# A four-layer macaron model on one Trainium2 core: ends of mixtures by tile, products ahead of the gates, and the first batch of layer 1's attention begun inside the mixture before it

## The chip, the core and the metric

The kernel runs on one core of one Trainium2 chip. The core has a matrix engine (PE, with its weight loads shown as PEld), a vector engine (DVE), a scalar engine (ACT), a general engine (POOL, or GpSimd) and a queue that issues most of the DMAs (SP). They run side by side and meet through semaphores; DMAs of all queues share 16 DMA engines. On-chip memory is SBUF (128 partitions) and PSUM (8 banks of 128 x 512 fp32 here), into which PE writes. The metric is the device time of one launch in microseconds (us); lower is better. Time before is the median of three runs.

## The reference, cut to what matters

The state x has 4 batches of 512 tokens of width 128, all in fp32. Every one of four layers adds half a mixture, an attention, and half a mixture again. In layers 1 and 2 the mixture is computed for every expert, in layers 0 and 3 by sending tokens to experts with a capacity.

```python
x = x + 0.5 * _L0_ffn_ref(_layernorm(x), ...)    # top 1, capacity 320, each layer: ffn, attn, ffn
x = x + _L0_attn_ref(_layernorm(x), ...)
x = x + 0.5 * _L0_ffn_ref(_layernorm(x), ...)
x = x + 0.5 * _L1_ffn_ref(_layernorm(x), ...)    # layer 1: the one that the change is mostly about
x = x + _L1_attn_ref(_layernorm(x), ...)
x = x + 0.5 * _L1_ffn_ref(_layernorm(x), ...)
...                                              # layer 2: dense mixture, scan, dense mixture
x = x + 0.5 * _L3_ffn_ref(_layernorm(x), ...)    # top 2, capacity 512
x = x + _L3_attn_ref(_layernorm(x), ...)
x = x + 0.5 * _L3_ffn_ref(_layernorm(x), ...)

def _L1_ffn_ref(x):                    # 8 experts of width 64, 2 shared ones (together 128 wide)
    shared = silu(x @ ws_gate.T) * (x @ ws_up.T) @ ws_down.T
    scores = sigmoid(x @ gate_weight.T)
    w, idx = top_k(scores, 2); w = 2.5 * w / (w.sum(-1) + 1e-20)
    return shared + sum over the two of w * expert(x)

def _L1_attn_ref(x):                   # 16 heads; scores are a product of two low-rank score matrices
    A1 = einsum('bnhr,bmhr->bhnm', q1, k1)   # rank 4
    A2 = einsum('bnhr,bmhr->bhnm', q2, k2)   # rank 8
    attn = softmax(causal(A1 * A2 * 32 ** -0.5))
    return (attn @ v) @ Wo.T + bo
```

## The kernel before

**Order of work.** The program is one straight sequence. Outside of marked blocks a scheduler arranges each engine's instructions by itself, from the order of the source and the dependences; inside blocks of `tc.manual_schedule` the named engines keep the order of the source. All attentions are such blocks (PE, DVE, ACT and POOL), and the chain from layer 1's second mixture to layer 3's first routing (the generator `behind`) is one for POOL alone. Work of two pairs of batches is interleaved by `skewed`: each stage is a generator that yields at step ends, and the second pair starts a given number of rounds after the first (5 for layer 1's first mixture, 8 for `behind`).

**Norms.** `norms` (from L155) takes statistics per tile of 128 tokens on DVE, `rs`, `rstd` (a power), and `off` on POOL (L164, L165, L168, L169) and the normalised tile on ACT, POOL or DVE (L174, L176, L178), as its argument `on` says. `normed_T` (L1039) uses it with "scalar", so ACT, for pairs of batches in the mixtures of layers 1 and 2.

**Mixtures with a capacity** (`Mixture`, layers 0 and 3: f00, f01, f30, f31). `experts` (from L414) goes over 8 experts. For each it makes the hidden rows `h` (L479, L483, L484), and then for every piece of 128 rows four products into one PSUM bank `po` (L514), a bias on DVE (`biased`, L496), a scale on ACT (L501) and an indirect scatter to DRAM by POOL (L502). `at_once` is how many pieces the bias takes at a time: all of them (`whole`), for the last expert one. `combine` (L524) loads the scattered rows of each batch (L529) and adds them to x (L530); in the last one the answer of each batch is sent out right behind (L1545).

**Layer 1's mixture** (`l1_ffn`, from L1075), for a pair of batches: normalise and turn (`normed_T`), gate scores (`scored`, Sigmoid at L1081), routing on DVE (`route`, `without`, up to the gates `comb` at L1094), the gates turned and written to DRAM (`to_rows`, L1065) and fetched back as rows replicated over partitions, 512 KB a piece, two per batch (`cb`, L1102, from SP). Then for each batch five steps k, the shared experts first: gate and up products on PE (L1127, L1128), Silu on ACT (L1130), times up on DVE (L1131), in the other steps times the gate rows on DVE (L1133), and, two steps behind, the down products of the step k - 2 (L1115). The result is added to x at L1140. The first step is of the shared experts, the other four of two experts each.

**Layer 1's attention** (`l1_attn`, from L1143). `begin(b)` normalises and turns batch b, makes three factor matrices (L1165), writes them to DRAM (L1172 once, L1176 eight times) and makes the values; `fetch` loads the factors replicated for a group of four heads (L1193), and `project` multiplies them to q on DVE and k on POOL (L1200), so that scores are one product per head (L600). Before the first score the tiles `vpad` for padded values are set to 0 and 1 on POOL (`padded_values`, L571, called at L796), and in layer 3 also the tiles `low` (L801).

**Layer 2's preparation** (`prep_l2`) turns `wo` of each expert on PE and copies the result on ACT (L1246, L1252), beside other work.

The main sequence is at L1466 to L1545.

Of the kernel before, what the change touches and what calls it, by code (L numbers as in the profile page):

```python
# [9 lines left out]
FP = mybir.dt.float32  # L10
# [31 lines left out]
def kernel(ctx: ExitStack, tc: tile.TileContext, a: dict, out: bass.AP):  # L42
# [109 lines left out]
    def norms(srcs, dsts, tag, on="vector", fine=False):  # L152
# [18 lines left out]
        for t in range(g):  # L171
            src, dst = srcs[t // NT][:, t % NT, :], dsts[t // NT][:, t % NT, :]
            if on == "scalar":
# [63 lines left out]
    class Mixture:  # L237
# [180 lines left out]
        def experts(self, w, beside=None):  # L418
# [3 lines left out]
            with tc.tile_pool(name=f"moe_{self.tag}", bufs=2) as pool:  # L422
# [47 lines left out]
                for e in range(E):  # L470
# [20 lines left out]
                    po = bank(f"o{tag}").rearrange("p (s d) -> p s d", d=D)  # L491
# [3 lines left out]
                    def biased(m, t0, t1):  # L495
                        nc.vector.tensor_tensor(  # L496
                            o[:m, t0:t1, :], po[:m, t0:t1, :], bc_mid(b2[:m, e, :], [m, t1 - t0, D]), ALU.add
                        )
# [11 lines left out]
                    at_once = 1 if e == E - 1 else whole  # L510
                    for s in range(per):
                        m = min(P, cap - s * P)
                        for c in range(NC):
# [4 lines left out]
                        if s >= whole or (s + 1) % at_once == 0:  # L518
                            first = s if s >= whole else s + 1 - at_once
                            biased(m, first, s + 1)  # L520
# [49 lines left out]

    def padded_values(pool):  # L571
        vpads.clear()
        for i in range(2):
            v = pool.tile([P, NT, NH, SLOT], FP, name=f"vpad{i}", tag=f"vpad{i}", bufs=1)
            nc.gpsimd.memset(v, 0.0)
            nc.gpsimd.memset(v[:, :, :, HD : HD + 1].rearrange("p t h o -> p (t h o)"), 1.0)
            vpads.append(v)

    def attention(pool, tag, begin, project, residual, owT, added, after=None, beside=(), fetch=None):
# [216 lines left out]
        padded_values(pool)  # L796
        if not added:
            lows = []
            for i in range(2):
                low = pool.tile([P, NT, P], FP, name=f"low{i}_{tag}", tag=f"low{i}", bufs=1)  # L800
                nc.gpsimd.memset(low, 0.0)  # L801
                lows.append(low)
# [236 lines left out]
    def normed_T(pool, bs, tag):  # L1039

        ns = [work.tile([P, NT, D], FP, name=f"n{b}_{tag}", tag="n", bufs=3) for b in bs]
        yield from norms([xs[b] for b in bs], ns, tag, "scalar")
# [32 lines left out]
    def l1_ffn(pool, i, bs):  # L1075
# [3 lines left out]
        plg = scored(nTs, l1["gate"], tag)  # L1079
        sc = pool.tile([P, G, E], FP, name=f"sc_{tag}", tag="sc1")  # L1080
        nc.scalar.activation(sc, plg, AF.Sigmoid)  # L1081
# [12 lines left out]
        nc.vector.tensor_tensor(comb, comb, bc(total, [P, G, E]), ALU.mult)  # L1094
        yield
# [11 lines left out]
        order = [NC] + list(range(NC))  # L1107
        for x, b in enumerate(bs):
            po = bank(f"o{b}_{tag}").rearrange("p (t d) -> p t d", d=D)
            hs = []  # L1110

            def down(k):

                for t in range(NT):
                    nc.tensor.matmul(  # L1115
                        po[:, t, :],
                        hs[k][:, t * P : (t + 1) * P],
# [5 lines left out]
            for k, c in enumerate(order):  # L1123
                gw = l1["wg"][:, c * P : (c + 1) * P] if c < NC else l1["sg"]
                uw = l1["wu"][:, c * P : (c + 1) * P] if c < NC else l1["su"]
                ps = pair(f"gu{c}_{b}_{tag}")
                nc.tensor.matmul(ps[0], gw, nTs[x], start=True, stop=True)  # L1127
# [454 lines left out]
```

## Time and profile before

| what | us |
|---|---|
| median of 3 runs | 1516.54 |
| lowest and highest of them | 1515.89, 1519.27 |
| the profiled execution | 1538.12 |
| its span, first to last instruction | 1536.2 |

The profiled execution is one run of its own, and 1.4% above the median. Its span is 1.9 us shorter than its time. Busy shares of its span:

| engine | busy us | share |
|---|---|---|
| PE | 1282.4 | 83% |
| DVE | 852.7 | 56% |
| ACT | 713.5 | 46% |
| POOL | 653.9 | 43% |

By the timeline the span divides into these stages:

| from to, us | stage |
|---|---|
| 60 to 112 | experts of layer 0's first mixture |
| 127 to 340 | layer 0's attention |
| 340 to 430 | routing and experts of layer 0's second mixture |
| 430 to 455 | norm and routing of layer 1's first mixture, end of layer 2's preparation |
| 455 to 514 | layer 1's first mixture |
| 514 to 533 | start of layer 1's attention, up to the first score |
| 533 to 755 | layer 1's attention |
| 757 to 832 | layer 1's second mixture |
| 832 to 1045 | layer 2, routing of layer 3's first mixture |
| 1045 to 1101 | experts of layer 3's first mixture |
| 1101 to 1416 | layer 3's attention |
| 1445 to 1518 | experts of layer 3's second mixture |
| 1518 to 1536 | loads of its rows, answers |

A line of the timeline has the start, the busy time, the engine, the line of the source, the operation, the tiles written and read, their shapes, the number of instructions, and in brackets the idle time of the engine before it with what ended it. A line of a group of instructions has the engine, the operation, tiles and shapes, the count, then the busy time of all and the mean in ns of one, then the idle time before them and what ended it.

### The profile page before, as it was taken

To read this page: it belongs to the slowest core of one execution; us is meant where nothing else is said; L and a number is where in the kernel's file an instruction comes from. 1 tells how busy PE (TensorE), PEld (TensorE's weight loads), DVE (VectorE), ACT (ScalarE), POOL (GpSimd) and SP (SyncE) were. 2 spreads that over 40 slices of the span, in tenths; PEclk is the share of its full clock that TensorE was granted. 3 is DMA by queue.
4 is the path that set the end of the run, shared out by engine and by line. 5 is a ranking of instruction groups with operands and counts; after the bars stand their busy time and mean duration, and the time that the engine had idled before them with its cause. 6 is when DMAs were issued, how large, how long until landed. Compare 5 with 4: busy or idle time off the path is not lost. (4 is left out here: it accounts for less than half of the span.)

```text
span 1536.2 us, 28724 instructions
## 1 busy us (share of the span) xinstructions
PE 1282.4 (83%) x10645; PEld 824.8 (54%) x10645; DVE 852.7 (56%) x2832; ACT 713.5 (46%) x1487; POOL 653.9 (43%) x776
## 2 busy tenths in 40 slices
PE   4788999996969689999799877829599999997493
PEld 3465666764756456667567656617443334332272
DVE  5226777663335367857456545434277787773342
ACT  1235877871443266777633232103236555564041
POOL 4356767761510287868401111544630224202253
PEclk9898999996979799999999868859879999999597
DMA  8420240002414575331050000032104000000233
GB/s 253 109 62 8 78 171 9 9 18 76 138 46 98 145 234 161 101 119 55 3 111 1 1 0 1 29 90 70 56 21 167 15 11 5 15 2 14 77 84 103
DMA packets 100659, 106.20 MB, mean 69 GB/s; under 512 B 9084, under 2 KB 73832, under 8 KB 100520
## 3 DMA queue, kind: packets, MB, share of 16 engines
q1 hardware_dynamic: 93864, 91.16, 20.6%
q0 software_dynamic: 6656, 13.22, 2.7%
q8 instruction: 84, 1.38, 0.4%
q14 instruction: 55, 0.45, 0.1%
HBM read 62.49 MB, written 41.85 MB: 68 GB/s over the span
## 5 line engine op out<-in xcount | busy, mean ns | idle before, releaser
L632 POOL TENSOR_SCALAR sc_a<-sc_a,top_a 128x128 f32<-128x128 f32 (+3 forms) x256 | 275.4, 1091 | 82.7 <-DVE top_a L617 54.5
L600 PE MATMUL s_a<-k_a,q_a 32*128 32x512 f32 (+3 forms) x1536 | 264.9, 549 | 20.8 <-DMA k_a<-fac_a 13.8
L709 ACT ACTIVATE w_a<-t_a 128x512 f32<-128x512 f32 x256 | 140.5, 596 | 121.8 <-PE t_a L600 89.8
L645 PE MATMUL t_a<-ident,sc_a 128*128 128x128 f32 x1280 | 173.0, 281 | 7.3 <-DVE top_a L621 6.9
L600 PE MATMUL t_a<-ql_a,k_a 32*128 32x512 f32 x512 | 168.7, 646 | 0.3 <-DVE low_a__12648 L689 0.2
L502 POOL DMA_INDIRECT res_f<-y_f,back_f x112 | 109.2, 975 | 139.6 <-ACT y_f L501 105.1
L645 PEld LDWEIGHTS t_a<-ident,sc_a 128*128 128x128 f32 x1280 | 143.8, 144 | 44.3 <-issue 16.6
L634 ACT ACTIVATE sc_a<-sc_a,top_a 128x128 f32<-128x128 f32 (+3 forms) x256 | 135.3, 575 | 27.8 <-DVE top_a L621 27.3
L600 PEld LDWEIGHTS s_a<-k_a,q_a 32*128 32x128 f32 x1536 | 92.7, 189 | 92.9 <-issue 41.3
L654 ACT ACTIVATE w_a<-t_a 128x256 f32<-128x256 f32 (+2 forms) x192 | 94.1, 526 | 70.3 <-PE t_a L645 70.0
L408 POOL DMA_INDIRECT disp_f<-n_f,to_f x96 | 95.1, 991 | 54.4 <-issue 36.7
L514 PE MATMUL o_f<-w_l,h_f 128*128 128x128 f32 (+1 forms) x896 | 113.4, 279 | 3.8 <-DVE o_f L496 1.7
L514 PEld LDWEIGHTS o_f<-w_l,h_f 128*128 128x128 f32 (+1 forms) x896 | 103.1, 184 | 15.1 <-DVE back_f L464 4.4
L479 PE MATMUL h_f<-dT_f,w_l 128*128 128x320 f32 (+1 forms) x256 | 105.1, 547 | 2.8 <-ACT dT_f L457 2.8
L164 POOL TENSOR_SCALAR rs_f<-mv_f 128x4 f32<-128x4 f32 (+1 forms) x23 | 5.8, 250 | 229.0 <-DVE mv_f L161 228.6
L667 PE MATMUL acc_a<-w_a,vpad 128*32 128x128 f32 x2560 | 98.0, 279 | 0.3 <-ACT w_a L654 0.3
L689 DVE TENSOR_REDUCE low_a__12648<-s_a 128x1 f32<-128x512 f32 x128 | 82.0, 684 | 26.3 <-PE t_a L600 18.9
L656 ACT COPY w_a<-t_a 128x256 f32<-128x256 f32 (+2 forms) x192 | 93.5, 526 | 6.5 <-PE t_a L645 6.4
L689 DVE TENSOR_REDUCE low_a__12646<-s_a 128x1 f32<-128x512 f32 x128 | 81.4, 684 | 21.9 <-PE t_a L600 15.6
L501 ACT ACTIVATE y_f<-o_f,d_f 128x128 f32<-128x128 f32 (+1 forms) x112 | 38.8, 394 | 112.4 <-DVE o_f L496 98.3
L621 DVE CUSTOM_DVE_ANT_0 sc_a<-s_a,future 128x128 f32<-128x128 f32 (+3 forms) x128 | 62.3, 487 | 48.8 <-PE s_a L600 40.9
L621 DVE CUSTOM_DVE_ANT_0 sc_a<-s_a,table 128x128 f32<-128x128 f32 (+3 forms) x128 | 62.3, 487 | 46.0 <-PE s_a L600 35.9
(343 smaller groups left out, 2274.3 us busy)
## 6 DMA issues: line engine op xcount, KB each, us to landing
fac_a<-fac_a_sb SPq DMA_DIRECT2D x36, 256.0 KB
disp_f<-zeros_f SPq DMA_DIRECT2D x4, 2080.0 KB
d_f<-disp_f SPq DMA_DIRECT2D x32, 260.0 KB
w_l<-in_L_ffn_w_dram SPq DMA_DIRECT2D x16, 512.0 KB
cb_f<-rows_f SPq DMA_DIRECT2D x16, 512.0 KB
q_a<-fac_a SPq DMA_DIRECT2D x32, 256.0 KB
k_a<-fac_a SPq DMA_DIRECT2D x32, 256.0 KB
r_f<-res_f SPq DMA_DIRECT2D x24, 256.0 KB
```

Source lines behind the costliest of these rows:

```text
L408: nc.gpsimd.indirect_dma_start(out=self.to[c][i0 + t][:, :], out_offset=bass.IndirectOffsetOnAxis(ap=to[:, c, t : t + 1], axis=0), in_=ns[ ...
L479: nc.tensor.matmul(ps[u][:, :cap], w1[:, e, (c + u) * P : (c + u + 1) * P], dT, start=True, stop=True)
L502: nc.gpsimd.indirect_dma_start(out=self.back[e * per + s][:, :], out_offset=bass.IndirectOffsetOnAxis(ap=back[:m, s : s + 1], axis=0), in_ ...
L514: nc.tensor.matmul(po[:m, s, :], h[:, c, s * P : s * P + m], w2[:, e, c, :], start=(c == 0), stop=(c == NC - 1),)
L600: nc.tensor.matmul(ps[:, n0:n1], q[r : r + SLOT, i * P : (i + 1) * P], k[r : r + SLOT, n0:n1], start=True, stop=True)
L621: nc.vector.tensor_tensor_reduce(sc, banks[r][:, :n], more, -1.0, HUGE, ALU.add, ALU.min, top)
L632: nc.gpsimd.tensor_scalar(sc, sc, top, None, ALU.subtract)
L634: nc.scalar.activation(sc, sc, AF.Exp, bias=top, scale=-1.0)
L645: nc.tensor.transpose(ps[:, x * n + j * P : x * n + (j + 1) * P], st["sc", u, i, r0 + x][:, j * P : (j + 1) * P], ident,)
L667: nc.tensor.matmul(st["acc", u][r * SLOT : (r + 1) * SLOT, i * P : (i + 1) * P], vpads[b % 2][:, j, g * 4 + r, :], st["w", u, i, r][:, j * ...
L689: nc.vector.tensor_reduce(st["low", u][:, i, c : c + 1], ps, AX.X, ALU.max, negate=True)
L709: nc.scalar.activation(w, ps, AF.Exp)
```

## The change

It has seven parts.

1. **Experts**: the last two experts get their PSUM bank per piece (per two pieces for the last but one) instead of one for all.
2. **Padded tiles**: `padded_values` and a new `rows_of_largest` are called ahead of layer 0's first and layer 3's first experts; in layer 1 one of the two tiles is made ahead of the mixture, the other when batch 1 begins.
3. **Layer 1's mixture**: the first two steps' gate and up products of a pair's first batch stand before and behind the routing (`up(0, 0)`, `up(0, 1)`); Silu becomes a Sigmoid on ACT and a multiply by the gate product on DVE; the multiply by the gate rows goes from DVE to POOL. A one-element Sigmoid runs ahead of layer 0's last combine.
4. **Layer 1's attention**: `begin` for batch 0, its fetches and its products q and k for two groups of heads follow the first pair's mixture in `followed`, and the second pair starts 12 rounds behind the first instead of 5.
5. **Norms** of `normed_T`: every second tile on ACT, the others on DVE ("both").
6. **Layer 2's preparation**: its copies go to ACT and DVE in turn (`copy`).
7. **Answers**: the last rows are loaded into eight own buffers, those of the first choice from SP and those of the second from ACT, before any of the adds and answers.
Layer 1's second mixture shares `l1_ffn`, so parts 3 and 5 apply there too.

```diff
-            if on == "scalar":
+            if on == "scalar" or (on == "both" and t % 2):
                 nc.scalar.activation(dst, src, AF.Identity, bias=off[:, t : t + 1], scale=rstd[:, t : t + 1])
...
-                    at_once = 1 if e == E - 1 else whole
+                    at_once = 1 if e == E - 1 else 2 if e == E - 2 else whole
                     for s in range(per):
                         m = min(P, cap - s * P)
+                        if s == 0 or (e >= E - 2 and s % at_once == 0):
+                            po = bank(f"o{s}_{tag}").rearrange("p (s d) -> p s d", d=D)
...
+    def padded(pool, i):
+        v = pool.tile([P, NT, NH, SLOT], FP, name=f"vpad{i}", tag=f"vpad{i}", bufs=1)
+        nc.gpsimd.memset(v, 0.0)
+        nc.gpsimd.memset(v[:, :, :, HD : HD + 1].rearrange("p t h o -> p (t h o)"), 1.0)
+        return v
...
-        yield from norms([xs[b] for b in bs], ns, tag, "scalar")
+        yield from norms([xs[b] for b in bs], ns, tag, "both")
...
+        order = [NC] + list(range(NC))
+        hs = {}
+
+        def up(x, k):
+            c = order[k]
...
+            nc.tensor.matmul(ps[0], gw, nTs[x], start=True, stop=True)
+            nc.tensor.matmul(ps[1], uw, nTs[x], start=True, stop=True)
+            h = pool.tile([P, S], FP, name=f"h{c}_{bs[x]}_{tag}", tag="h1", bufs=6)
+
+            nc.scalar.activation(h, ps[0], AF.Sigmoid)
+            nc.vector.tensor_tensor(h, h, ps[0], ALU.mult)
+            nc.vector.tensor_tensor(h, h, ps[1], ALU.mult)
+            hs[x, k] = h
+
+
+        up(0, 0)
         yield
         m1, s1 = route(pool, sc, G, "0")
...
         nc.vector.tensor_tensor(comb, comb, bc(total, [P, G, E]), ALU.mult)
+        up(0, 1)
         yield
...
             for k, c in enumerate(order):
-                h = pool.tile([P, S], FP, name=f"h{c}_{b}_{tag}", tag="h1", bufs=6)
-                nc.scalar.activation(h, ps[0], AF.Silu)
-                nc.vector.tensor_tensor(h, h, ps[1], ALU.mult)
+                if (x, k) not in hs:
+                    up(x, k)
                 if c < NC:
-                    nc.vector.tensor_tensor(h, h, cbs[x][:, c, :], ALU.mult)
+                    nc.gpsimd.tensor_tensor(hs[x, k], hs[x, k], cbs[x][:, c, :], ALU.mult)
...
             def begin(b):
+                if b == 1:
+                    vpads[1] = padded(pool, 1)
+                if b > 0:
+                    yield from begin_(b)
 
             def fetch(b, g):
+                if (b, g) not in early:
+                    fetch_(b, g)
 
             def project(b, g):
+                return early[b, g] if (b, g) in early else project_(b, g)
...
-            nc.scalar.copy(woT, ps)
+            copy(woT, ps)
...
+        padded_values(tables)
         f00.experts(l0["w"])
...
+        first = small.tile([P, 1], FP, name="first_sigmoid", tag="first_sigmoid", bufs=1)
+        nc.scalar.activation(first, l2["m"][:, 0, 0:1], AF.Sigmoid)
         for b in range(NB):
             whole(f01.combine(b))
-        with tc.tile_pool(name="ffn10", bufs=2) as pool:
-            whole(skewed([l1_ffn(pool, 0, bs) for bs in pairs], 5))
+        with tc.tile_pool(name="ahead1", bufs=2) as ahead:
+            vpads[:] = [padded(ahead, 0), None]
+            begun = l1_begin(ahead)
+
+            def followed(pool, bs):
+                yield from l1_ffn(pool, 0, bs)
+                if bs[0] == 0:
+
+                    yield from begun[0](0)
+                    for g in range(2):
+                        begun[1](0, g)
+                        yield
+                        begun[4][0, g] = begun[2](0, g)
+
+            with tc.tile_pool(name="ffn10", bufs=2) as pool:
+                whole(skewed([followed(pool, bs) for bs in pairs], 12))
...
+    with tc.tile_pool(name="answers", bufs=1) as pool:
+        rs = [[pool.tile([P, NT, D], FP, name=f"r{j}{b}_last", tag=f"r{j}{b}") for j in range(2)] for b in range(NB)]
+        for b in range(NB):
+            for j, queue in enumerate((nc.sync, nc.scalar)):
+                row = 1 + j * T + b * S
+                queue.dma_start(rs[b][j], f31.res[row : row + S, :].rearrange("(t p) d -> p t d", p=P))
+        for b in range(NB):
+            for r in rs[b]:
+                nc.vector.tensor_tensor(xs[b], xs[b], r, ALU.add)
+            nc.sync.dma_start(out_view[b], xs[b])
```

`l1_begin` holds the former `begin`, `fetch` and `project` of `l1_attn` unchanged, with the tile `future`.

## The prediction

> **What bounds the kernel now.** I read the clock and span first (one core, 1536.2 us, mean clock 0.902), then the windows of busy time by stage, then the timeline in each stretch where PE is idle, and the groups of instructions last for durations. The whole-span shares (PE 83%, POOL 43%) average over stages with different limits, so the windows decide.
>
> ```profile
> core 0: us, PE busy (x) PEld busy (x) DVE busy (x) ACT busy (x) POOL busy (x), PEclk, DMA share, GB/s
> 425.00:455.00 30.00, 18.07 (x109) 15.87 (x110) 10.18 (x53) 14.38 (x34) 5.54 (x9) 0.75 0.12 36
> 455.00:513.00 58.00, 56.66 (x272) 36.63 (x271) 31.44 (x68) 19.29 (x30) 2.54 (x3) 0.98 0.35 74
> 513.00:533.00 20.00, 5.13 (x29) 3.29 (x32) 3.36 (x5) 2.42 (x3) 6.17 (x7) 0.72 0.74 216
> 545.00:755.00 210.00, 196.84 (x2500) 138.90 (x2495) 137.66 (x582) 153.37 (x337) 157.32 (x157) 0.98 0.38 118
> 770.00:800.00 30.00, 29.75 (x141) 18.84 (x140) 17.25 (x45) 11.51 (x19) 0.00 (x0) 1.00 0.49 103
> 1515.00:1537.00 22.00, 0.00 (x0) 0.00 (x0) 5.83 (x9) 0.40 (x1) 0.96 (x1) 0.58 0.52 149
> ```
>
> Numbers after a window are its length, then busy time per engine. Where PE is full (455–513, 545–755, 770–800) only less or better fed PE work helps. Where PE is empty the path runs through DMAs and small operations: 513–533, between layer 1's first mixture and its attention, and the end. The first hole in the timeline:
>
> ```profile
> 511.78 2.00 PE L1115 MATMUL o_f<-wd1T,h_f 128*128 128x128 f32 x16
> 517.32 0.35 SPq L1172 DMA_DIRECT2D fac_a<-fac_a_sb  x1
> 517.87 5.64 SPq L1176 DMA_DIRECT2D fac_a<-fac_a_sb  x8
> 531.48 1.26 POOL L1200 TENSOR_TENSOR k_a<-k_a,k_a 128x512 f32<-128x512 f32 x1 [12.61 <-DMA k_a<-fac_a]
> 532.79 5.67 PE L600 MATMUL s_a<-k_a,q_a 32*128 32x128 f32 x32 [13.84 <-DMA k_a<-fac_a]
> ```
>
> The last product ends at 513.78 and the first score starts at 532.79: 19.0 us, of which 15.5 (517.3 to 532.75) are one chain: factors written to DRAM, fetched replicated, multiplied.
>
> **Layer 1's attention begun early: −14.** Normalising, turning, three factors and values of batch 0 (about 5 us of PE: 0.60 turn, 3×0.86, 0.9 and gaps), their 9 writes and 8 fetches on SP, and the products q and k (0.69 DVE, 1.26 POOL) now follow pair 0's mixture inside pair 1's. If the factors leave for DRAM 15.5 us before pair 1 ends, scores start about 0.4 us behind the last product. The instruction order puts q and k behind the fourth batch's last gate multiply; replayed with the durations above, 17 to 18.6 us are left, so the cover is 1 to 2 us thin. SP's queue holds pair 1's gate-row loads ahead of the factors, nothing behind that PE needs. PE's own 5 us move, they don't vanish: the mixture runs 455–513.8 now and has to hold them.
>
> The mixture changes too. Per step k, PE has 1.72 us of gate and up products and 0.88 of down products: 2.61 us. Elementwise rows of before:
>
> ```profile
> L1131 DVE TENSOR_TENSOR h_f<-h_f,gu_f 128x512 f32<-128x512 f32 x40 | 27.5, 687 | 42.9 <-PE gu_f L1128 29.0 <-ACT h_f L1130 13.6
> L1133 DVE TENSOR_TENSOR h_f<-h_f,cb_f 128x512 f32<-128x512 f32 x32 | 21.5, 688 | 2.3 <-DMA cb_f<-rows_f 1.8
> L1200 POOL TENSOR_TENSOR k_a<-k_a,k_a 128x512 f32<-128x512 f32 x16 | 20.4, 1276 | 17.7 <-DMA k_a<-fac_a 15.3 <-DVE top_a L617 2.4
> ```
>
> Silu becomes Sigmoid and one more DVE multiply (40 × 0.69 = 27.5 us of DVE), the gate multiply goes from DVE (32 × 0.688) to POOL (32 × 1.28): DVE is even, POOL gets 41 us. Per k DVE has 1.38, POOL 1.28, both under PE's 2.61. From the end of the gate and up products to the down product 5.2 us of other PE work stand in between; the chain is 0.60 + 0.69 + 0.69 + 1.28, about 3.7 with handovers. So in steady state it costs nothing: the cover is 1.5 us.
>
> Here **a rule speaks against the change**. The Trainium skill, "GPSIMD Engine Reference", section 4.1, says not to put two-input elementwise work on GpSimd, about twice as slow as VectorE. The rows agree on the ratio (1276 to 688, 1.85). Taken as time on the path the rule would cost 32 × 0.59 = 19 us and eat the whole gain; by the windows POOL has 2.54 us of work in 58 and 0.00 in 30, so the price falls only where PE waits for the product: at each pair's start, after the gate rows land. Going by the rows I charge it there only. A second rule, "SBUF — State Buffer", section "SBUF: two separate sides": GpSimd reading SBUF and a VectorE operation with two SBUF inputs exclude each other for a whole instruction. DVE's two products in a step read one input from PSUM, so by the rule itself few pairs collide; no row of before shows such a collision, and I take 0, up to 16 × 0.3 in the range.
>
> At each pair's start: gate rows take 8.7 us from issue at 457.18 to first use at 465.85. Before, PE filled that with the first steps; now two of these stand in front of the gates (up(0,0), up(0,1): 3.4 us), so PE is fed during the route (its 18.07 of 30 in 425–455) but has 3.4 us less to do afterwards. Four DVE multiplies (2.8 us) stand inside the route, 1.5 of it late. Replayed: stalls of 1.9 and 3.1 us in pair 0, 1 and 1.8 in pair 1. Table loads of 1.28 us, four or five in this mixture now, nearly all go; after the first products they lie on the path (456.56, 465, 467). Mixture end with PE's 5 us inside: 516 to 518.5; scores about 518.8 against 532.8, **−14**, between −9 (factors 5 us late) and −17.
>
> **Second layer-1 mixture: +6.** It stands in POOL's hand-fixed order, which is empty now:
>
> ```profile
> 767.82 2.59 SPq L1102 DMA_DIRECT2D cb_f<-rows_f  x4
> 775.57 1.89 DVE L1133 TENSOR_TENSOR h_f<-h_f,cb_f 128x512 f32<-128x512 f32 x3
> ```
>
> Three multiplies ran at once on DVE when the rows landed (1.89 us). On POOL they take 3 × 1.28, and then pair 1's norm (0.25 + 1.67 + 0.25 + 0.2 = 2.4 us, L164–169) stands in front of the fourth. The route's comb is ready at about 766.9 for 764.5, rows land at 778 for 775.6, the fourth multiply ends at 785.6, so batch 1's products start at 787.6 for 780.9; the pair after that at 822.9 for 815.4: +7. Four saved table loads give 1 back: **+6**, from 0 (layer 2's waits behind absorb it; the clock of 0.70–0.81 there shows PE idle) to +9.
>
> **Mixtures' ends by tile: −7.2.** The last expert's pieces share one PSUM bank now and PE waits for DVE's read of each; POOL's scatters, 1.27 us apart, follow the products:
>
> ```profile
> 1511.28 1.16 PE L514 MATMUL o_f<-w_l,h_f 128*128 128x128 f32 x8 [0.38 <-issue]
> 1515.96 0.29 DVE L496 TENSOR_TENSOR o_f<-o_f,b_l 128x128 f32<-128x128 f32 x1 [3.19 <-remote]
> 1516.96 0.96 POOL L502 DMA_INDIRECT res_f<-y_f,back_f  x1 [2.46 <-ACT y_f L501]
> ```
>
> With a bank per piece, and the seventh expert's scatters in pairs (the first 2.1 us earlier), POOL's row of eight closes up; the last scatter starts 1514.2 for 1516.96: −2.8, and likewise in layer 3's first mixture (1097.0 for 1099.80): −2.8. If the unexplained 1.9 us ahead of the last bias stays, −2.7 (POOL is the limit then anyway). In layer 0's mixtures (cap 320, three pieces) the same reasoning gives −0.6 and −1.0.
>
> **Padded tiles moved: +1.** In layer 0's and layer 3's attention the memsets (1.8 us each, L575) stand beside a DVE wait that ends later (POOL was free at 1107.43, its next input came at 1109.09), so 0 although the timeline shows 3.55 us of memset there. In layer 1's, vpad 1 now stands in POOL's order among the first scores, where POOL is 75% busy (157.32 of 210): 0 to 2, I take +1.
>
> **Norms on two engines: −3.** Eight ACT normalisations of 0.40 (3.2 us, 762.58) become four and four on DVE of about 0.3: 1.5 us shorter per norm. In layer 1 other work covers it; in layer 2's latency-bound stretch (880–1000, clock 0.70–0.81) some of it shows: 0 to −6. **Copies of wo2's preparation alternate: 0 ± 1**; 0.57 us ACT against 0.69 DVE per expert, in a chain of 2.3.
>
> **The answers: −2.** Eight loads and four outputs after the last scatter took 1519.2 to 1536.2. Two queues and own buffers let all loads start at once. Against this stands the Trainium skill, "Trainium Kernel Development and Optimization", section "Key Constraints": queues share 16 DMA engines, more issuers save only issue time. The row: 1527–1532 moved 271 GB/s at a DMA share of 0.93, 1519–1523 182 at 0.62. By the row alone at its best rate 3.15 MB take 11.6 us, with 2 us to the first landing and 0.7 at the end 14.3: −2.7. By the rule nothing but issue gaps goes: 0 to −1. I take −2, from 0 to −4.
>
> **Sum** −14 + 6 − 7.2 (2.8 + 2.8 + 0.6 + 1.0) + 1 − 3 − 2 = −19.2, against the profiled execution's own 1538.12 (span 1536.2 and 1.9 outside). That execution is 1.4% above the median of 1516.54; scaled by 0.986 the change is −18.9: **1497.6**. About 0.2% (3 us) is what a measurement of this kernel tells from no change.
>
> **Rivals.** (A) As summed, 1489 to 1507: 0.55. (B) The early start is mostly given back: POOL's pace holds both mixtures (factors and tails of 5 us in the first, +11 in the second): −19.2 + 10 = −9, 1507.5. For it: the thin cover of 1.5 us per step and the 1 to 2 us in front of the scores; against it POOL's emptiness. 1507 to 1513: 0.18. (C) The second mixture loses nothing since PE is idle in layer 2 anyway, layer 2 gains its 5: −19.2 − 6 − 2 = −27, 1490 and below: 0.15. (D) Slower: **gate rows uncovered**. The place is the start of each pair in both mixtures, four in all; with the first two products spent ahead of the gates PE meets the second down product with nothing else queued, and stands for the whole landing and multiply, 8.7 + 1.3 = 10 us. Four times is 40 us where the sum has about 16, so +24: −19.2 + 24 = +5, 1521. It decides from (19.2 + 3 + 16) / 4 = 9.6 us of stall a pair on. For it: products are in program order on PE; against it: two more gate-and-up products and a down (4.3 us) still stand ahead. 0.07. (E) The change's early begin doesn't hide the chain, since factor DMAs share the engines with 4 MB of gate rows, and the second mixture loses 9: −19.2 + 12 + 3 + 2 = −2, 1514.5: 0.05, within 3 us.
>
> Range: 1487 to 1512 leaves D, E and the far end of C out. Faster: A, B, C, 0.88; the same 0.05; slower 0.07.
>
> **What the profile after would show.** Scores within 2 us of the last down product of layer 1's first mixture, no DMA as releaser; its last product 2.5 to 5 us later than 513.8 (stage start unmoved). Second mixture: PE waiting for POOL's h at batch 0's second to fourth steps and POOL's pow in front of the fourth. The last eight scatters of both k = 2 mixtures 1.27 apart without a gap. The end 14 to 16 us behind the last scatter. Wrong would be: q or k released by a DMA long after the mixture; second mixture unlengthened; a POOL gap kept in front of the last scatter.

## The result and the profile after

| | before | after |
|---|---|---|
| median of 20 runs each, us | 1516.11 | 1513.15 |
| lowest and highest | 1513.89, 1519.38 | 1507.94, 1517.43 |
| profiled execution, span | 1536.2 | 1511.3 |

The ratio is 0.9976, with a 95% interval of 0.9967 to 0.9985: 3.6 us faster (the medians differ by 3.0), where 18.9 were forecast. The two profiles show 24.9 us, and most of that is not the change. The kernel before alone had medians of 1533.6, 1518.7, 1515.8, 1519.0 and 1516.2 us in the five sessions below (a session is a set of kernels timed together on one chip; the expectations say call), the first and the third of them on the same chip. Within a session the mean granted clock of an execution goes along with its time (1528 us at 0.909 and 1544 at 0.897). Between sessions it does not explain the difference (two profiles of before span 1533.9 us at 0.904 and 1516.5 at 0.905), and the cause stays open. So only runs of one session are compared, and stages are read from profiles taken in one session, unless the text says otherwise.

Windows of the kernel after, in two of the places shown of before (length, then busy time per engine, clock, DMA share and rate):

```profile
core 0: us, PE busy (x) PEld busy (x) DVE busy (x) ACT busy (x) POOL busy (x), PEclk, DMA share, GB/s
513.00:533.00 20.00, 14.52 (x111) 9.33 (x110) 12.33 (x57) 9.17 (x19) 18.32 (x18) 0.91 0.45 118
770.00:800.00 30.00, 28.50 (x120) 18.11 (x120) 17.76 (x44) 8.26 (x15) 5.47 (x5) 0.91 0.28 60
```

The hole of 513–533 is gone: PE 14.52 instead of 5.13. The timeline there, PE and POOL:

```profile
511.25 1.95 PE L1135 MATMUL o_f<-wd1T,h_f 128*128 128x128 f32 x16
514.45 1.26 POOL L1213 TENSOR_TENSOR k_a<-k_a,k_a 128x512 f32<-128x512 f32 x1
514.54 1.16 PE L1135 MATMUL o_f<-wd1T,h_f 128*128 128x128 f32 x8 [1.34 <-POOL h_f L1147]
515.76 4.74 PE L610 MATMUL s_a<-k_a,q_a 32*128 32x128 f32 x32
```

The first score starts 0.06 us behind the last product's end, and no DMA releases it. The early start works as forecast. The loss is in the second mixture, where PE stands twice for POOL, and POOL stands idle until the gate rows land (PE's lines first, then the end of the second pair's statistics on DVE, then POOL's):

```profile
758.91 1.02 PE L1093 MATMUL gu_f<-nT_f,wu1T 128*128 128x512 f32 x2
763.00 3.61 PE L1135 MATMUL o_f<-wd1T,h_f 128*128 128x128 f32 x24 [3.06 <-POOL h_f L1147]
769.55 2.08 PE L1135 MATMUL o_f<-wd1T,h_f 128*128 128x128 f32 x8 [2.94 <-POOL h_f L1147]
771.42 1.91 PE L187 MATMUL T_f<-ident,n_f 128*128 128x128 f32 x8
743.43 0.29 DVE L161 BATCH_NORM_AGGREGATE mv_f<-st_f 128x2 f32<-128x6 f32 x2
761.68 3.71 POOL L1147 TENSOR_TENSOR h_f<-h_f,cb_f 128x512 f32<-128x512 f32 x3 [19.03 <-DMA cb_f<-rows_f]
765.48 0.25 POOL L164 TENSOR_SCALAR rs_f<-mv_f 128x8 f32<-128x8 f32 x1
765.82 1.67 POOL L165 TENSOR_TENSOR rstd_f<-rs_f,mhalf 128x8 f32<-128x8 f32 x1
768.15 1.35 POOL L1147 TENSOR_TENSOR h_f<-h_f,cb_f 128x512 f32<-128x512 f32 x1
```

These lines show which work waits for which: the second pair's norm (L164, L165) could run as soon as its statistics are there (L161, done at 743.72), but it stands in POOL's queue behind three multiplies that wait for the rows, and runs at 765.48. Its tiles are turned (L187) only at 771.42, behind the first pair's down products. In the kernel before (its profile from experiment 1's second session, whose layer 1 ends 10 us later) the norm follows its statistics, the tiles are turned before the down products, and these don't wait:

```profile
753.75 0.25 POOL L164 TENSOR_SCALAR rs_f<-mv_f 128x8 f32<-128x8 f32 x1 [1.16 <-DVE mv_f L161]
771.33 0.82 PE L187 MATMUL T_f<-ident,n_f 128*128 128x128 f32 x6
771.98 3.74 PE L1115 MATMUL o_f<-wd1T,h_f 128*128 128x128 f32 x32
```

Stages of single profiled executions, cut at events that all kernels share (scores of layer 1: first to last; mixture 2: from there to its last down product; layer 2: to its last product; experts 3: to the last scatter of layer 3's first mixture; layer 3: the attention to its last score; last experts: to the last scatter). The first three columns are from one session, the fourth from a later one, in which the second mixture of the kernel after takes 103.8 us:

| stage, us | before | after | multiply on DVE | norm early |
|---|---|---|---|---|
| start to first score of layer 0 | 126.5 | 127.5 | 126.7 | 127.2 |
| to last scatter of layer 0 | 294.9 | 295.4 | 293.8 | 293.7 |
| to first score of layer 1 | 106.9 | 96.3 | 93.7 | 93.3 |
| scores of layer 1 | 207.9 | 210.7 | 210.4 | 210.6 |
| mixture 2 | 91.3 | 101.1 | 92.0 | 93.6 |
| layer 2 | 147.9 | 145.8 | 144.9 | 146.7 |
| experts 3 | 111.7 | 109.7 | 109.7 | 109.3 |
| layer 3's scores | 283.3 | 283.2 | 283.2 | 283.3 |
| last experts | 127.8 | 125.9 | 125.9 | 126.6 |
| answers | 18.2 | 16.8 | 16.5 | 16.4 |
| span | 1516.5 | 1512.4 | 1496.9 | 1500.7 |

### The profile page after: what moved, and what is told of

Read it like the earlier page. It is cut to its first block, busy times and chain, and to the rows that moved or that the text cites. A ratio compares the mean times of both kernels' runs of the same rounds, so it can differ in the third digit from the quotient of the medians.

```text
span 1511.3 us, 28774 instructions
## 1 busy us (share of the span) xinstructions
PE 1271.2 (84%) x10645; PEld 816.7 (54%) x10645; DVE 880.3 (58%) x2890; ACT 682.8 (45%) x1431; POOL 694.0 (46%) x808
## 4 chain that ended last, share of the span: by engine, by line
PE 70%; DVE 9%; POOL 8%; DMA 5%; issue 5%; ACT 3%; SPq 1%; POOLq 0%; ACTq 0%; DVEq 0%
PE s_a L610 13%; PE t_a L655 10%; PE o_f L515 6%; PE h_f L479 6%; PE acc_a L677 5%; PE acc_a L749 5%; PE y_f L1329 3%; PE t_a L610 3%; POOL disp_f L408 2%; PE ot_a L768 2%; PE gu_f L1092 2%; PE lg_f L322 1%; POOL rstd_f L165 1%; DVE low L699 1%; PE gu_f L1093 1%
## 5 line engine op out<-in xcount | busy, mean ns | idle before, releaser
L699 DVE TENSOR_REDUCE low<-s_a 128x1 f32<-128x512 f32 x256 | 163.4, 684 | 45.4 <-PE t_a L610 32.7
L655 PEld LDWEIGHTS t_a<-ident,sc_a 128*128 128x128 f32 x1280 | 144.6, 144 | 41.0 <-issue 16.5
L515 PE MATMUL o_f<-w_l,h_f 128*128 128x128 f32 (+1 forms) x896 | 109.6, 277 | 0.0
L1147 POOL TENSOR_TENSOR h_f<-h_f,cb_f 128x512 f32<-128x512 f32 x32 | 40.7, 1286 | 104.4 <-DVE h_f L1098 62.7
L631 DVE CUSTOM_DVE_ANT_0 sc_a<-s_a,table 128x128 f32<-128x128 f32 (+3 forms) x128 | 62.3, 487 | 43.5 <-PE s_a L610 38.3
L749 PE MATMUL acc_a<-w_a,vpad 128*32 128x256 f32 x1024 | 82.1, 391 | 1.0 <-DVE low L699 0.9
## 6 DMA issues: line engine op xcount, KB each, us to landing
disp_f<-zeros_f SPq DMA_DIRECT2D x4, 2080.0 KB, 10.6
```

The source lines that it names most:

```text
L515: nc.tensor.matmul(po[:m, s, :], h[:, c, s * P : s * P + m], w2[:, e, c, :], start=(c == 0), stop=(c == NC - 1),)
L631: nc.vector.tensor_tensor_reduce(sc, banks[r][:, :n], more, -1.0, HUGE, ALU.add, ALU.min, top)
L655: nc.tensor.transpose(ps[:, x * n + j * P : x * n + (j + 1) * P], st["sc", u, i, r0 + x][:, j * P : (j + 1) * P], ident,)
L699: nc.vector.tensor_reduce(st["low", u][:, i, c : c + 1], ps, AX.X, ALU.max, negate=True)
L749: nc.tensor.matmul(acc[r * SLOT : (r + 1) * SLOT, n0:n1], vpads[b % 2][:, j, g * 4 + r, :], st["w", u, j, r][:, n0:n1], start=(j == 0 and ...
```

## The experiments

Each was timed in five rounds (the second run in one) beside the kernel before on the same chip; intervals are 95%, and ratios are to before.

**1. Before and after once more.** No edit; the first run in a first session, the second and third in another, the fourth in a later one.

> The kernel before, unchanged, for a second profile of it. Theory one (the first profile of before, 1538 us, was a slow execution, 22 us above the median, and its gap ahead of layer 1's attention or its later stages are longer than in a usual one): ratio 1.000, and a profiled execution of about 1516 us in which some stage is some 20 us shorter than in the first profile. Theory two (the profile lengthens this kernel each time, the kernel after not): the second profile is near 1538 us too, with the same 19.0 us between the last down product and the first score.

> The kernel before unchanged, for a profile taken on the same chip as the kernel after in this call. Theory one (the stages that the change touches are worth 10 to 13 us in every execution, and the rest of the difference between the first two profiles was the chip): ratio 1.000, and stage by stage the same as in its other profiles, with only the attentions' lengths and the clock changed. Theory three (in executions on a chip that grants more clock, the gap in front of layer 1's attention and layer 2 are shorter too): these stages shorter by some us than 104 us (last scatter of layer 0 to first score of layer 1) and 376 us (last score of layer 1 to first score of layer 3).

> The kernel after, unchanged, beside before on one chip. Theory one (local gains of some 13 us, given back as lower granted clock in the long attentions): ratio 0.998, with the attentions longer than before's by about 10 us in the profiles of this call. Theory two (the gains were the chip's): ratio 0.998, attentions equal, and the stages between them shorter by only 3 us.

> The kernel after, unchanged, in the same call as the run with the early norm, so that the two are told apart on one chip: ratio to before 0.997.

Before: 1.0014 [1.0001, 1.0028] and 0.9997 [0.9983, 1.0011], spans 1533.9 and 1516.5. The first expectation's account of a single odd execution falls: the profile's 1535.7 us are usual for its session, whose median is 1533.6. After: 0.9969 [0.9956, 0.9982] and 0.9963 [0.9948, 0.9979]. On one chip the attention of layer 3 is of equal length (283.3 and 283.2 us). Those of layers 0 and 1 are longer in the kernel after, first to last score: 205.0 for 203.4 us at a mean granted clock of 0.98 for 1.00, and 210.7 for 207.9 at 0.96 for 0.97. So something is given back there, less than the 10 us of the first theory; what lowers the clock is not shown. Compared on one chip, 10.6 us come out ahead of layer 1's first score and 9.9 go in the second mixture.

**2. Parts of the change alone on the kernel before**: the padded tiles and the early begin with the old mixture; and the mixtures' ends with the answers.

```diff
-            whole(skewed([l1_ffn(pool, 0, bs) for bs in pairs], 5))
+                whole(skewed([followed(pool, bs) for bs in pairs], 12))
...
-                    at_once = 1 if e == E - 1 else whole
+                    at_once = 1 if e == E - 1 else 2 if e == E - 2 else whole
```

> The kernel before with the padded tiles moved and the early begin of layer 1's attention alone (second pair 12 rounds behind, the first batch's factors inside the first mixture), mixtures as before. Theory one (the early start is worth its 13 us and the mixtures in their new form give it back): ratio about 0.991, -13 us. Theory two (the 19 us gap is much shorter in a usual execution or the pairs set apart cost as much): ratio 0.997 to 1.000.

> The kernel before with the mixtures' ends by tile and the answers' loads into own buffers, nothing else. By the two profiles these are worth 2.5 (layer 0) + 3.0 + 2.4 (layer 3) + 2.1 (answers) = 10 us: ratio 0.9934 if they hold outside the profile; 0.998 to 1.000 if POOL's scatters and the DMAs take their time anyway.

Early begin alone: 0.9974 [0.9962, 0.9987], 4 us. Its stage up to layer 1's first score is 97.4 us against 104.4 of before in that session, so 7: with the pairs 12 rounds apart and nothing ahead of the gates, the second pair's first product comes 16.5 us later (487.13 for 470.68), 1.9 of it lost at the start of layer 0 (experiment 6).

Ends and answers alone: 1.0008 [0.9994, 1.0022], nothing. The last scatter of layer 0's second mixture comes 42.5 us after its first instead of 43.5, and then the mixture of layer 1 waits longer. PE before (first fence) and with the new ends (second):

```profile
438.61 1.16 PE L1249 MATMUL m<-wo2T,raw 128*128 128x128 f32 x8 [0.78 <-ACT wo2T L1246]
439.61 1.04 PE L187 MATMUL T_f<-ident,n_f 128*128 128x128 f32 x8
```

```profile
441.32 1.16 PE L1250 MATMUL m<-wo2T,raw 128*128 128x128 f32 x8 [0.79 <-ACT wo2T L1247]
442.31 1.04 PE L187 MATMUL T_f<-ident,n_f 128*128 128x128 f32 x8
```

The stalls that the new ends take out of the experts had been filled with layer 2's preparation (L1249). Now one of its steps more stands in front of layer 1's transposes: T_f comes 2.7 us later, though the last scatter here ends only 0.5 us later (423.68 for 423.23).

**3. The new form of the mixture**: old in both uses; old in the second use alone.

In the second kernel `l1_ffn` is before's, and the new one has another name:

```diff
-                yield from l1_ffn(pool, 0, bs)
+                yield from l1_ffn_new(pool, 0, bs)
```

> The kernel after with layer 1's mixture (both uses) in its old form: Silu, gate multiply on DVE, no products ahead of the gates; all other parts kept. Theory one (the new form costs about 14 us in the second mixture and nothing in the first): ratio to before about 0.988, -18 us. Theory two (the new form is neutral): ratio 0.998, as the kernel after.

> The kernel after with layer 1's mixture in its new form in the first use alone, the old form in the second. Theory one: last score of layer 1 to first score of layer 3 about 371 us instead of 378, ratio to before about 0.994. Theory two (layer 2 behind is bound by its own waits): 0.998.

Old in both: 0.9984 [0.9967, 1.0001]; old in the second alone: 0.9903 [0.9884, 0.9921]. So the new form is worth having in the first mixture (the stage up to layer 1's first score is 101.0 us with the old form and 95.7 with the new, where before took 104.4 and 106.9 in these two sessions) and costs about 9 us in the second (92.4 against 101.1). The first expectation's "costs nothing in the first" had the sign wrong.

**4. Which part of the form: the multiply by the gate rows.** Back on DVE (twice, in different sessions); moved to POOL in the kernel before as the only edit; only the fourth of each batch in the second mixture on DVE.

```diff
-                    nc.gpsimd.tensor_tensor(hs[x, k], hs[x, k], cbs[x][:, c, :], ALU.mult)
+                    nc.vector.tensor_tensor(hs[x, k], hs[x, k], cbs[x][:, c, :], ALU.mult)
```

> The kernel after with the multiply by the gate rows back on DVE, all else kept. Theory one (POOL's queue, with pair 1's norm in front of the fourth multiply, makes the second mixture 8 us longer up to its second batch): the second batch's first product 38.5 instead of 46.8 us after layer 1's last score, ratio to before about 0.993. Theory two (layer 2 takes up what the mixture loses): the same stage shorter, the time equal to the kernel after's, 0.998.

> The kernel after with the gate multiply on DVE once more, in one call with the version that puts back two parts beyond it: ratio to before 0.990, as in its first run; nearer to 0.987 if that run was a slow draw.

> The kernel before with one edit: the multiply by the gate rows on POOL in both mixtures. Theory one (the multiply on POOL costs about 12 us wherever it stands): ratio 1.006 to 1.008, the second mixture 5 to 9 us longer. Theory two (it is dear only together with products ahead of the gates and the extra DVE multiply): 1.000 to 1.002.

> The kernel after with only the fourth gate multiply of each batch in the second mixture on DVE, so that none stands behind the second pair's norm in POOL's fixed order; the other twelve there and all of the first mixture stay on POOL. Queue theory (the norm's 2.4 us in front of the fourth multiply, and what stands behind it, make most of the loss): the second mixture 6 us shorter than the kernel after's 101 us, ratio to before about 0.993. Duration theory (1.28 for 0.69 us on twelve of sixteen multiplies is the loss): 2 us shorter, ratio 0.996.

On DVE: 0.9903 [0.9881, 0.9925] and 0.9902 [0.9883, 0.9921], 15 to 17 us faster than before; against the kernel after in the same session (1502.0 for 1514.09) 12 us, 9.1 of it in the second mixture. On POOL in the kernel before: 1.0030 [1.0017, 1.0042], 4.2 us slower. There the norm is caught as well (L164 at 769.36, behind three multiplies, for 753.75), and the second mixture takes 96.0 us where before takes 90.2 to 91.3 in other sessions. So it costs about 5 us alone and about 10 in the kernel after, which has spent two steps of products ahead of the gates; that these are the reason for the other 5 is likely and was not tested. The fourth alone on DVE: 0.9953 [0.9937, 0.9969], and the second mixture still 100.1 us, beside 101.1, 103.7 and 103.8 in three profiles of the kernel after. That is the queue theory as I had put it in the prediction (the fourth multiply behind the norm), and it falls: freeing the fourth multiply frees 1 to 4 us. In the profile with the multiply on DVE the norm's place in time gives the lead:

```profile
742.27 0.25 POOL L164 TENSOR_SCALAR rs_f<-mv_f 128x8 f32<-128x8 f32 x1 [1.16 <-DVE mv_f L161]
760.78 1.04 PE L187 MATMUL T_f<-ident,n_f 128*128 128x128 f32 x8
761.66 1.02 PE L1092 MATMUL gu_f<-nT_f,sg1T 128*128 128x512 f32 x2
765.08 1.10 PE L1092 MATMUL gu_f<-nT_f,sg1T 128*128 128x512 f32 x2
766.25 2.49 DVE L1147 TENSOR_TENSOR h_f<-h_f,cb_f 128x512 f32<-128x512 f32 x4
767.74 2.50 PE L1135 MATMUL o_f<-wd1T,h_f 128*128 128x128 f32 x21
```

The second pair's norm is on POOL at 742, right after its statistics, not at 765. So while the rows come, PE turns the second pair's tiles, makes its gate scores and the first products of two more batches, and needs the down products only at 767.74.

**5. The order alone.** The multiplies stay on POOL; the norm's four operations are recorded ahead of them.

```diff
-            yield from l1_ffn(pool, 1, bs)
+            step = l1_ffn(pool, 1, bs)
+            if bs[0]:
+                next(step)
+                for _ in range(4):
+                    yield
+            yield from step
...
-                whole(skewed([behind(pool, bs) for bs in pairs], 8))
+                whole(skewed([behind(pool, bs) for bs in pairs], 5))
```

> The kernel after with one change of order: in the second mixture, POOL's four operations of the second pair's norm stand ahead of the first pair's gate multiplies instead of behind the third; the multiplies stay on POOL. Blocked-norm theory (the norm waits on POOL behind multiplies that wait for the gate rows, so PE has nothing of the second pair to do meanwhile): from layer 1's last score to the mixture's last product about 94 us instead of 101, and ratio to before 0.991 to 0.993. Duration theory (1.28 for 0.69 us a multiply[...]): 100 us, ratio 0.996 to 0.997.

0.9897 [0.9873, 0.9922], against 0.9963 [0.9948, 0.9979] of the kernel after in the same session: 1503.0 for 1512.6 us, the second mixture 93.6 for 103.8 us.

```profile
741.46 0.25 POOL L164 TENSOR_SCALAR rs_f<-mv_f 128x8 f32<-128x8 f32 x1
758.88 1.04 PE L187 MATMUL T_f<-ident,n_f 128*128 128x128 f32 x8
761.12 4.96 POOL L1147 TENSOR_TENSOR h_f<-h_f,cb_f 128x512 f32<-128x512 f32 x4 [16.95 <-DMA cb_f<-rows_f]
764.97 3.29 PE L1135 MATMUL o_f<-wd1T,h_f 128*128 128x128 f32 x28
```

Four multiplies of 1.24 us are on POOL as ever, and PE does not wait for them. This is shown, then: the 10 us were the norm caught in POOL's fixed order behind multiplies that wait for a transfer. All of the second pair hangs on it. Counted from layer 1's last score (first three columns of one session):

| us until | before | after | multiply on DVE | norm early |
|---|---|---|---|---|
| the second pair's tiles are turned (T_f) | 35.1 | 44.5 | 36.0 | 34.1 |
| its gates are turned (gT_f) | 49.2 | 59.2 | 52.7 | 49.8 |

The two stands of PE are 5 to 6 us of the loss; the rest is this pair's later routing. What the longer duration costs is at most the small rest (93.6 against 92.0, one profile each).

**6. The small parts, on the kernel with the multiply on DVE**: the ends and answers old; the ends old in layer 0 alone; the norms on ACT alone; layer 0's padded tiles behind its experts; and ends old in layer 0 with norms on ACT.

```diff
-                    at_once = 1 if e == E - 1 else 2 if e == E - 2 else whole
+                    at_once = 1 if e == E - 1 else 2 if e == E - 2 and self.k == 2 else whole
...
-        yield from norms([xs[b] for b in bs], ns, tag, "both")
+        yield from norms([xs[b] for b in bs], ns, tag, "scalar")
...
-        padded_values(tables)
         f00.experts(l0["w"])
+        padded_values(tables)
```

> The kernel after with the gate multiply on DVE (as in the run before) and the mixtures' ends and the answers in the old form. If these two parts are worth the 6.7 us that the two profiles of one chip show (1.1 in layer 0's second mixture, 2.1 and 2.0 in layer 3, 1.5 in the answers): ratio to before about 0.9947, against 0.9903 with them. If they are worth nothing, as with the kernel before: 0.990.

> The kernel after with the gate multiply on DVE and the mixtures' ends by tile in layer 3 alone, layer 0's two mixtures in the old form. If the new end in layer 0's second mixture costs 3 us net (its last scatter comes 1.3 us earlier, but layer 2's preparation, which filled the gaps on PE, then stands in front of layer 1's first products): ratio 0.987 to 0.988, below the 0.990 and 0.9916 of that kernel with all ends new. Otherwise 0.990.

> The kernel after with the gate multiply on DVE and the norms of the dense mixtures on ACT alone, as before. If the split of the norms is worth the 2 to 3 us that layer 2 lost in the profile: ratio 0.992 to 0.993. If not: 0.990.

> The kernel after with the gate multiply on DVE and the padded tiles of layer 0 recorded behind its first experts instead of ahead of them. Theory one (their memsets stand among POOL's first work and make layer 0's routing 1 to 2 us later): first score of layer 0 about 1.3 us earlier than with them ahead, ratio 0.989 to 0.990. Theory two (the start is bound by the DMAs): no change, 0.990.

> The kernel after with three parts put back: the gate multiply on DVE, layer 0's mixtures with their old end, and the dense mixtures' norms on ACT alone. If the three are worth their single differences (12, about 5 and about 3 us): ratio to before about 0.983. If the two small ones were the scatter of few runs: 0.987 to 0.990, as the kernel with the multiply on DVE in this call.

| kernel | ratio to before | up to first score of layer 1 | layer 2 | span |
|---|---|---|---|---|
| multiply on DVE, two runs | 0.9903, 0.9902 | 93.7, 93.6 | 144.9, 144.8 | 1496.9, 1496.2 |
| ends and answers old | 0.9877 [0.9852, 0.9901] | 89.4 | 144.9 | 1499.0 |
| ends old in layer 0 | 0.9850 [0.9828, 0.9871] | 91.6 | 145.0 | 1496.7 |
| norms on ACT | 0.9876 [0.9854, 0.9897] | 90.7 | 148.6 | 1498.7 |
| padded tiles behind | 0.9916 [0.9895, 0.9937] | 93.3 | 144.8 | 1496.2 |
| ends old in layer 0, norms on ACT | 0.9919 [0.9898, 0.9940] | 94.6 | 146.1 | 1504.5 |

By single profiles, the new ends in layer 0 give back 2 to 4 us in the stage that follows, and split norms take 3.7 us out of layer 2 and put 3 into layer 1's front; but in three profiles of the kernel after that front stage spreads from 93.2 to 96.3 us. Neither pays clearly. The last row, meant as the best of all, is not (one of its six executions took 2411.74 us and is left out). Its two parts don't add; that each changes the order which the scheduler makes for the whole front is a guess (its second mixture is 93.9 us, its scores of layer 1 212.4).

The padded tiles' edit tested nothing: the scheduler put the two memsets among POOL's first work all the same, at 7.20 and 12.11 us, for 7.20 and 12.07 without the edit. What their new place costs shows in experiment 2's early begin, which touches nothing else ahead of layer 0's attention. The first line is before's, the second the early begin's (the other memset is at 12.28):

```profile
112.42 3.55 POOL L575 MEMSET vpad<- 128x2048 f32 x2 [1.94 <-DMA res_f<-y_f,back_f]
7.20 1.80 POOL L573 MEMSET vpad<- 128x2048 f32 x1
```

POOL's powers and token numbers of the first routing stand between and behind them now, and layer 0's first scatter comes at 68.6 us for 66.7 of before in that session, the first score at 127.3 for 125.4. In the five profiles with the old place that scatter comes at 66.7 to 67.7 us, in the fifteen with the new one at 68.3 to 70.1. So this part costs 1 to 2 us at the start.

The best version measured is the one with old ends in layer 0: 1496.0 us, from five runs in one session, and its profile is no shorter than that with the multiply alone put back, so more than the latter's 1501 to 1502 us is not claimed.

## Why the prediction was wrong

The forecast's terms beside what the columns "before" and "after" of one session give for them:

| term | forecast, us | measured, us |
|---|---|---|
| early start, first mixture | -14 | -10.6 |
| second mixture | +6 | +9.9 |
| ends in layer 0 (first to last scatter, both mixtures) | -1.6 | -1.4 |
| padded tiles (start, to layer 0's first scatter) | 0 | +1.7 |
| layer 0's scores | 0 | +1.6 |
| ends in layer 3 | -5.6 | -3.9 |
| padded tiles (layer 1's scores) | +1 | +2.8 |
| norms (layer 2) | -3 | -2.1 |
| answers | -2 | -1.4 |
| sum | -19.2 | -4.1 (span) |

Small differences between these stages make up the rest of the sum. The direction was right, the size was a fifth of the forecast, and every term came out on its dear side.

- **Second mixture: the step that failed**, by its reason and as the largest single miss; +9.9 lies beyond the +9 given as its far end, and in the two other profiles of after the stage is longer still (103.7 and 103.8 us for 101.1). The prediction saw that norm and multiplies share POOL's fixed order, and asked only what the norm does to the fourth multiply (2.4 us). That much came true: batch 1's first product comes 45.4 us behind layer 1's last score for 39.6, so +5.8 where it had +6.7. It didn't ask what the first three multiplies do to the norm: they wait for the gate rows, the norm behind them waits too, and with it all of the second pair (its gates 10 us late, the fourth batch's first product 9.3 us, where the forecast had 7.5). With the order mended the stage is 93.6 us and with the multiply on DVE 92.0, so the loss was not the price of a multiply but of an order, and the whole change would then have come near its forecast (15 to 17 us instead of 18.9).
- **Early start**: the mechanism was right, down to q and k behind the last gate multiply, with no DMA in front of the scores. The first down product (of the shared experts) already comes 2.9 us later than before's (38.7 us after layer 0's last scatter for 35.7), ahead of any multiply on POOL; that is where most of the 3.4 is missing. In the first profile of after the whole stage is 93.2 us, which is 13.7 less than in the first of before. PE runs as many products in both profiles of after; its mean granted clock in the stage is 0.89 in the one of 96.3 us and 0.98 in the one of 93.2, so most of the miss goes with the clock. A slip of its own: 17 to 18.6 us for a chain of 15.5 leave 1.5 to 3.1 us, not 1 to 2.
- **The rule on GpSimd** against elementwise work there (the Trainium skill, "GPSIMD Engine Reference", section 4.1) was set aside on the argument that POOL is empty. As a price it would have been 19 us; 12 were measured (experiment 4), so the rule's advice would have served better here than my sum. But its reason, the doubled duration, is not what cost most: with the order mended the same multiplies make the second mixture 1.6 us longer than on DVE (93.6 for 92.0). An empty engine is not a free one if its order is fixed and the new work waits.
- **Ends by tile**: in layer 3 the forecast took 1.9 us of unexplained wait ahead of the last bias for a fixed part of the end. It is in before's first profile and not in the one of the session compared here, whose last bias and scatter follow (the bias waits 1.25 us for PE, as the two before it do). Nor does POOL's row of eight close up: in the kernel after 2.71 us lie between the fourth and the fifth scatter, 1.26 between the others. In layer 0 the scatters' own gain is as forecast (43.0 to 42.5 and 43.5 to 42.5 us), but the work of layer 2's preparation, which filled those stalls, is late next, as experiment 2 shows.

```profile
1496.25 0.29 DVE L496 TENSOR_TENSOR o_f<-o_f,b_l 128x128 f32<-128x128 f32 x1 [1.25 <-PE o_f L514]
1497.25 0.96 POOL L502 DMA_INDIRECT res_f<-y_f,back_f  x1 [0.52 <-ACT y_f L501]
```

- **Padded tiles**: they were taken out of a place where they cost nothing and put in front of layer 0's routing, which costs 1 to 2 us and was not asked; it is the second mixture's mistake once more. The 2.8 us in layer 1's scores are not explained by them: the early begin of experiment 2 has both the moved tiles and the early fetches, and its scores take 209.8 us for 209.6 of before in that session. **Layer 0's scores**: PE runs the same 2473 products there; the 1.6 us come with the lower granted clock (0.98 for 1.00), whose cause is not shown. **Norms**: near in layer 2; that they cost something in front of layer 1 was not counted, and is only indicated. **Answers**: between the rule (0 to -1) and the best rate (-2.7).
- **Rivals.** The fourth, gate rows uncovered at a pair's start, named the place, and PE does stand there (3.06 and 2.94 us at the first pair of the second mixture). The first of these is the landing that it feared, a third as long; the second is the norm's. The fifth came out nearest in size (-2 for -3.6): its second mixture losing 9 is what happened, its factors landing late is not. The second put the loss down to POOL's pace, which is not what made it.

## What to carry to other kernels

When work is moved to an engine whose order is written by hand, ask of each moved instruction two questions: what it will wait for, and what that is ready stands behind it in that queue. A short operation that releases another engine's work must stand ahead of one that waits for a transfer. And a stall taken out of an engine was often filled by work for later; look where that work goes before counting the stall as gain.

## What else the runs showed

With the fourth multiply on DVE and the first three on POOL, the two engines' products with both inputs in SBUF met:

```profile
762.49 4.16 POOL L1147 TENSOR_TENSOR h_f<-h_f,cb_f 128x512 f32<-128x512 f32 x3 [20.48 <-DMA cb_f<-rows_f]
762.82 1.48 DVE L1147 TENSOR_TENSOR h_f<-h_f,cb_f 128x512 f32<-128x512 f32 x1
```

DVE's took 1.48 us instead of 0.69, and POOL's three 4.16 instead of 3.71 (the second of them 1.72 instead of 1.27). This agrees with the Trainium skill, "SBUF — State Buffer", section "SBUF: two separate sides", by which such a product on DVE and one on GpSimd shut each other out. In the kernel after, where DVE's products read PSUM, POOL's stay at 1.26 to 1.35 us in the second mixture, so the 0 that the prediction took for this was right there; in the first mixture one of sixteen, beside DVE's product q, takes 1.58. But its reading that no row of before shows such a collision was wrong. The product q, with both inputs in SBUF, has a row of its own, and its mean is not 688 ns:

```profile
L1200 DVE TENSOR_TENSOR q_a<-q_a,q_a 128x512 f32<-128x512 f32 x16 | 13.5, 843 | 15.2 <-DMA q_a<-fac_a 15.2
```

Eight of the sixteen take 0.94 to 0.96 us instead of 0.69, and each of them starts while a POOL operation that reads SBUF (L632, 1.57 us) runs. They are done before it is, so DVE was not shut out for the whole of that operation, as the page has it.
